# Selections of a graph layer's edge groups issued one step sooner, with half the descriptor store for POOL's gathers

## The chip, the cores and the metric

The kernel runs on one core of a Trainium2 chip. Its time is the device time of one execution in microseconds (us). Three runs of the kernel before took 1988.96, 1992.68 and 1994.04 us; their median is 1992.68. The engines are called PE (matrix products; PEld is its weight load), DVE (vector operations), ACT (activations and copies), POOL (here it only issues gathers) and SP (here it only issues DMAs). A queue name with a q, such as SPq, is an engine's list of DMA issues.

## The reference, cut to what matters

One message-passing layer on a graph of 12,500 nodes with 64 features and 200,000 edges with 32 features, the edges sorted by destination. All is float32.

```python
msg_in = concatenate([nodes[row], nodes[col], edge_features], axis=-1)   # 200000 x 160
messages = relu(msg_in @ mW1 + mb1) @ mW2 + mb2                          # hidden 128, out 64
aggregated = segment_sum(messages, col, num_segments=12500)
upd_in = concatenate([nodes, aggregated], axis=-1)
y = relu(upd_in @ uW1 + ub1) @ uW2 + ub2
out = layernorm(nodes + y)                                               # over 64 features
```

Here `row` is the source (`src`) and `col` the destination (`dst`) of an edge.

## The kernel before, in words

**Tiles, steps, supers.** An edge tile is 128 edges; there are 1563. A *step* `s` is 8 tiles (`SUB`), 196 steps in all; a *super* `g` is 16 tiles (`SUP`), two steps, 98 in all. In a step, `g, j = divmod(s, 2)`: j says whether it is the first or second step of its super.

**Tables.** The first product is split: `A = x @ mW1[source part]` and `B = x @ mW1[destination part] + mb1` are made once for all nodes and kept in DRAM (`tab_a`, `tab_b`). `chunk_a` makes 1024 rows of A: PE (L410), a copy by ACT (L420, half) and DVE (L418, half) into a tile `tb` with two buffers, and a DMA from ACT's queue (L422). There are 13 such pieces. The first 7 steps gather rows of x itself and multiply them (L236, L269); all later steps gather rows of A, so the first of those gathers waits until all 13 pieces are written.

**A step.** `gather(s)` issues 8 indirect DMAs on POOL (L168), each fetching the 128 source rows of a tile into `xg` (14 buffers). `edge_part(s)` lets PE compute the other two parts (L255): the left operand `l` holds, for each edge, its 32 edge features and a 32-row one-hot of its destination within a window of 32 nodes; the right operand `rhs` holds the weights of the edge features and the 32 rows of B of that window, which `windows(s)` fetches with 8 DMAs on SP (L229). `node_part(s)` adds the gathered rows (DVE L276) and applies the ReLU (ACT L277). `collect(s)` lets PE sum the messages by destination (L302) with the one-hot `sel` (edges x 32 nodes), and count edges (L307) with `selb`, its bfloat16 copy. Every few steps a period of up to 448 nodes is closed, updated, normalised and stored (`close`, `update`, `residual`, `norm`, `store`, with PE L337 to L347, ACT L339, DVE L351 to L364, SP L370).

**What a super's selection is.** `loadd(g)` fetches the destinations of 2048 edges into the one-hot rows of `l` (SP L184; three such operands in turn). `select(g)` runs on DVE: the node numbers (L194), the one-hot rows of `l` in place (L196), and `sel` (L200). `load(g)` fetches the edge features into the other rows of `l` (SP L215, two DMAs); for g > 2 it has to wait for L196, which writes all rows. `counts(g)` is ACT's copy to `selb` (L208). `sel` and `selb` come from the pool `sup`.

**What sets the order.** The order is written out by hand (`tc.manual_schedule()`): each engine runs its instructions in the order in which the loop `for s in range(last + 3)` issues them, and waits by semaphores. Before the loop the start issues 7 steps of gathers, the weights, the tables with some preparation put between pieces (`if k == ...`), and `relative`, which turns destinations into places within a window (L380). DMAs of SP and ACT complete on eight semaphores handed out in turn; each such DMA waits until the one that had its semaphore before has landed. POOL's gathers rotate over eight others in the same way.

In the kernel before, the loop issues `select`, `load` and `counts` of super g + 1 in the first step of super g, and `loadd` of super g + 2 in its second step. The store in SBUF for the descriptors of POOL's DMAs is set in the constructor at L779 (`dynamic_dma_scratch_size`), 32,768 bytes of each partition.

Of the kernel before, what the change touches and what calls it, by code (L numbers as in the profile page):

```python
# [26 lines left out]
NSUP = -(-NT // SUP)  # L27
# [39 lines left out]
def gnn_kernel(ctx: ExitStack, tc: tile.TileContext, x1T, x, eT, e_rows, src, dst, dst_row, wrow, wnext, whalf,  # L67
# [24 lines left out]
    nc = tc.nc  # L92
# [56 lines left out]
    def frees(s):  # L149

        a = (XG + 1) // 2 + s - XG - ROWB
        return min(2 * a + 1, XG - 1) if a < (XG + 1) // 2 else XG + a - (XG + 1) // 2
# [17 lines left out]
                in_offset=bass.IndirectOffsetOnAxis(ap=src_s[:, t:t + 1], axis=0))  # L170
        xg[s] = buf, a

    with tc.tile_pool(name="sup", bufs=2) as sup, tc.tile_pool(name="work", bufs=2) as work, tc.manual_schedule():
        L, S, SB, xs, hs, pcs, sums = {}, {}, {}, {}, {}, {}, {}
        pt = psum.tile([P, SUB // 2, P], F32, name="pt", tag="sums")

        def loadd(g):

            l = operand[g % 3]
            o = g * SUP * P  # L180
            dv = dst_row[:, o:o + SUP * P].rearrange("o (k b e) -> o b k e", b=2, e=P)
            for b in range(2):
                q = 64 * b + SK
                nc.sync.dma_start(l[q:q + WIN].bitcast(I32), dv[:, b].broadcast_to([WIN, SUP // 2, P]))  # L184
            L[g] = l

        def select(g):


            nt = min(SUP, NT - g * SUP)  # L190
            l = L[g]
            c = WIN + SUP // 2 * (g % 2)
            node = cps[:, c:c + SUP // 2]
            nc.vector.tensor_scalar(node, wh[:, g * SUP // 2:(g + 1) * SUP // 2], pidx, None, op0=ALU.add)  # L194
            for r in ([slice(0, P)] if g > 2 else [slice(SK, SK + WIN), slice(64 + SK, 64 + SK + WIN)]):
                nc.vector.tensor_tensor(l[r], l[r].bitcast(I32),  # L196
                                        node[r].unsqueeze(2).broadcast_to([r.stop - r.start, SUP // 2, P]),
                                        op=ALU.is_equal)
            s = sup.tile([P, SUP, WIN], F32, name="sel")
            nc.vector.tensor_tensor(s[:, :nt], slot.unsqueeze(1).broadcast_to([P, nt, WIN]),  # L200
                                    drc[:, g * SUP:g * SUP + nt].unsqueeze(2).broadcast_to([P, nt, WIN]),
                                    op=ALU.is_equal)
            S[g] = s

        def counts(g):
            nt = min(SUP, NT - g * SUP)
            sb = sup.tile([P, SUP, WIN], BF, name="selb")
            nc.scalar.copy(sb[:, :nt], S[g][:, :nt])  # L208
            SB[g] = sb

        def load(g):

            for b in range(2):
                q = 64 * b + EK
                nc.sync.dma_start(L[g][q:q + DE], eT[g, b])  # L215

        def windows(s):

            g = s // (SUP // SUB)
            o = s % (SUP // SUB) * SUB  # L220
            nt = len(tiles(s))
            r = rhs[g % 2]
            tab, n = (B0, EARLY - WIN + 1) if g < GE else (B, N)
            _, ws = nc.values_load_multi_w_load_instructions(
                wint[0:1, s * SUB:s * SUB + nt], engines=[ET.SP], min_val=0, max_val=n - 1,
                skip_runtime_bounds_check_because="destinations are node numbers")
            for i in range(nt):
                q = SK + 64 * (i % 2)
                nc.sync.dma_start(r[q:q + WIN, (o + i) // 2, :], tab[bass.ds(ws[i], WIN), :])  # L229
# [88 lines left out]
        def close(u):  # L318

            ps, pn = sums.pop(u)  # L320
            nc.scalar.copy(sums_s[u % 2], ps)  # L321
            nc.scalar.copy(xw[u % 2][0:1, :UW], pn)
# [52 lines left out]
        def relative(a, b):  # L375

            wbc = work.tile([P, WCH], I32, name="wbc", tag="tb")
            nc.sync.dma_start(dst_s[:, a:b], dst[:, a:b])
            nc.sync.dma_start(wbc[:, :b - a], wrow[:, a:b].broadcast_to([P, b - a]))
            nc.vector.tensor_tensor(drc[:, a:b], dst_s[:, a:b], wbc[:, :b - a], op=ALU.subtract)  # L380
# [33 lines left out]
        def chunk_a(c):  # L414
            pb, tb = products(c, w1a)
            for h, m in spread(c):
                if h:
                    nc.vector.tensor_copy(tb[:, h, :m], pb[:, h, :m])  # L418
                else:
                    nc.scalar.copy(tb[:, h, :m], pb[:, h, :m])  # L420
            n = min(NCH, NB - c)
            nc.scalar.dma_start(Av[:, c:c + n, :], tb.rearrange("p h i f -> p (h i) f")[:, :n])  # L422

        def chunk_b(c, into):
            pb, tb = products(c, w1b)
            n = min(NCH, NB - c)
            pf, tf = (t.rearrange("p h i f -> p (h i) f")[:, :n] for t in (pb, tb))
            nc.vector.tensor_tensor(tf, pf, b1.unsqueeze(1).broadcast_to([P, n, DH]), op=ALU.add)
            for v in into:
                nc.sync.dma_start(v[:, c:c + n, :], tf)  # L430

        def offsets():

            nc.vector.memset(usup[:, 0:1], 0)
            wv = wint.rearrange("o (s t) -> o s t", t=SUB)
            ov = woff.rearrange("o (s t) -> o s t", t=SUB)
            k = 0
            while k < K:
                end = UPD[k + 1:] + [NSUB]
                d = end[0] - UPD[k]  # L440
                n = 1
                while k + n < K and k and end[n] - UPD[k + n] == d:
                    n += 1
                if k:
                    nc.vector.tensor_copy(usup[:, k:k + n], wv[:, UPD[k]:UPD[k] + (n - 1) * d + 1:d, 0])
                w, o = (v[:, UPD[k]:UPD[k] + n * d].rearrange("o (n d) t -> o n (d t)", n=n) for v in (wv, ov))
                nc.vector.tensor_tensor(o, w, usup[:, k:k + n].unsqueeze(2).broadcast_to([1, n, d * SUB]),
                                        op=ALU.subtract)
                k += n
            nc.vector.tensor_tensor(ustep[:, 1:], usup[:, 1:], usup[:, :-1], op=ALU.subtract)  # L450
            for v in (woff, ustep[:, 1:]):
                nc.vector.tensor_scalar(v, v, 0.0, float(UW - WIN), op0=ALU.max, op1=ALU.min)
# [31 lines left out]
        for k, c in enumerate(range(0, NB, NCH)):  # L484
            chunk_a(c)
            if k == 0:
                chunk_b(0, [B0v, Bv])
            if k == 2:

                w0 = wint[:, :GE * SUP]  # L490
                nc.vector.tensor_scalar(past, w0[:, GE * SUP - 1:], float(EARLY - WIN), None, op0=ALU.is_gt)
                nc.vector.tensor_scalar(w0, w0, float(EARLY - WIN), None, op0=ALU.min)
                windows(0)
                windows(1)
            if k == 4:
                relative(0, 8 * SUP)
            if k == 6:
                offsets()
            if k == 9:
                select(0)  # L500
                load(0)
                counts(0)

        def rest(s):

# [77 lines left out]
        for s in range(last + 3):  # L583
            g, j = divmod(s, SUP // SUB)
            while gathered < NSUB and frees(gathered) < s:
                gather(gathered)
                gathered += 1
            if s - 2 in due:
                norm(due[s - 2])
            if s + 2 < NSUB:  # L590
                windows(s + 2)
            if s < NSUB:
                node_part(s)
            if 1 <= s <= NSUB:
                collect(s - 1)
            if s + 1 in due:
                close(due[s + 1])
            if j == 0 and g + 1 < NSUP:
                select(g + 1)
                load(g + 1)  # L600
                counts(g + 1)
            if j == 1 and g + 2 < NSUP:
                loadd(g + 2)
            if chunks and s >= BS and chunks[0] < NCH + NB * (s + 1 - BS) / (SUP // SUB * (GE - 1) - BS):
                chunk_b(chunks.pop(0), [Bv])
            if s + 1 < NSUB:
                if s + 1 < XG:
                    transpose(s + 1)
                edge_part(s + 1)
            if s in due and due[s] + 1 < K:  # L610
                carry(due[s] + 1)
            if s in due:
                update(due[s])
            if s - 1 in due:
                residual(due[s - 1])
            if s + 2 in due:
                columns(due[s + 2])
            rest(s)
            if s - 2 in due:
                store(due[s - 2])  # L620
# [166 lines left out]
```

## Time and profile before

| | |
|---|---|
| median of three runs | 1992.68 us |
| the profiled execution | 1992.68 us, its span 1990.9 us |
| granted TensorE clock, mean | 0.537 |
| gathers from the table (POOL L168) | 1507, 0.944 us each, first at 85.4, last at 1966.4 |
| `select`: DVE L196 / L200 | 98 supers, 1.22 us (128 rows) / 0.68 us |
| ACT L208 | 98, 0.62 us |
| adding gathered rows (DVE L276) | 190, 1.22 us; idle ahead of it 1185.6 us in all |

Busy shares are averages over the whole span. "Idle before" is time in which an engine did nothing just ahead of an instruction, put down to what ended it; for an engine that does not set the pace it costs nothing. A line `A <- B: us, times, longest` says that A waited for B. In a timeline, a row is start, duration, engine, line, operation, tiles, count, and in brackets the idle time ahead of it. Times are from the start of the span.

### The profile page before, as it was taken

How to read it: one execution, taken by the hardware profiler on the slowest of the kernel's cores; microseconds unless marked ns; L12 is line 12 of the kernel's file. 1: busy time of each engine (PE TensorE's matmuls, PEld its weight loads, DVE VectorE, ACT ScalarE, POOL GpSimd, SP SyncE). 2: the span in 40 equal slices, each digit the busy share in tenths (PEclk: the TensorE clock that was granted, in tenths of full speed). 3: DMA queues.
4: the chain of work that ended last, by engine and by line, in shares of the span. 5: the costliest groups of instructions: out<-in, count | busy, mean ns of one | idle time of the engine just before them, and what ended most of it. 6: DMA issues, size and time to landing. Idle time of an engine off the chain costs nothing. (4 is left out here: it accounts for less than half of the span.)

```text
span 1990.9 us, 34069 instructions
## 1 busy us (share of the span) xinstructions
PE 1446.1 (73%) x9234; PEld 1276.3 (64%) x9234; DVE 538.9 (27%) x1013; ACT 342.0 (17%) x453; POOL 1477.4 (74%) x1572
## 2 busy tenths in 40 slices
PE   3688666765766766767767767777778778888797
PEld 2577666665655655656666666666667667767675
DVE  1424222222221222222222222222222223232222
ACT  0221111111111111111111111111111112121121
POOL 7577777777777777777777777777777777777773
PEclk8575555555555555555555555555555555555555
DMA  8645444433333333333333433333334333334341
GB/s 208 178 122 138 117 119 110 110 95 93 96 96 95 96 96 98 97 95 98 97 97 97 100 96 100 97 101 97 100 96 104 98 100 100 102 100 105 97 105 50
DMA packets 240741, 208.75 MB, mean 105 GB/s; under 512 B 76605, under 2 KB 207167, under 8 KB 240560
## 3 DMA queue, kind: packets, MB, share of 16 engines
q0 software_dynamic: 50016, 100.70, 20.6%
q1 hardware_dynamic: 175998, 96.93, 17.8%
q10 hardware_dynamic: 14546, 8.93, 1.7%
q8 instruction: 87, 1.43, 0.3%
q14 instruction: 94, 0.77, 0.1%
HBM read 188.50 MB, written 17.83 MB: 104 GB/s over the span
## 5 line engine op out<-in xcount | busy, mean ns | idle before, releaser
L168 POOL DMA_INDIRECT xg<-tab_a,src_s x1507 | 1423.0, 944 | 471.4 <-issue 448.3
L302 PEld LDWEIGHTS sums<-sel,h 128*128 128x128 f32 x3126 | 650.9, 315 | 362.5 <-ACT h L277 325.9
L302 PE MATMUL sums<-sel,h 128*128 128x32 f32 x3126 | 661.2, 385 | 296.4 <-ACT h L277 292.1
L276 DVE TENSOR_TENSOR h<-pc,xg 128x1024 f32<-128x1024 f32 (+1 forms) x190 | 230.8, 1215 | 1185.6 <-DMA xg<-tab_a,src_s 1163.2
L255 PE MATMUL pc<-rhs,l 64*128 64x128 f32 x3126 | 398.4, 426 | 94.2 <-DVE h L276 87.2
L277 ACT ACTIVATE h<-h 128x1024 f32<-128x1024 f32 (+1 forms) x190 | 199.2, 1049 | 1264.9 <-DVE h L276 1258.2
L255 PEld LDWEIGHTS pc<-rhs,l 64*128 64x128 f32 x3126 | 341.6, 314 | 111.4 <-DVE h L276 91.6
L196 DVE TENSOR_TENSOR l<-l,cps 128x1024 f32<-128x1024 int32 (+1 forms) x101 | 123.3, 1221 | 36.5 <-DMA l<-in_dst_row 23.9
L346 PE MATMUL py<-ux,xw 128*128 128x64 f32 x272 | 86.8, 422 | 28.4 <-DVE h L276 28.4
L337 PE MATMUL pu<-sums_s,w2u 128*128 128x448 f32 x68 | 63.3, 1034 | 55.5 <-DVE h L276 55.0
L346 PEld LDWEIGHTS py<-ux,xw 128*128 128x128 f32 x272 | 71.8, 323 | 36.9 <-DVE h L276 32.0
L347 PE MATMUL py<-u,hTu 128*128 128x64 f32 x272 | 85.5, 418 | 0.4 <-ACT hTu L339 0.4
L208 ACT CAST selb<-sel 128x512 bf16<-128x512 f32 x98 | 60.4, 616 | 104.0 <-DVE sel L200 100.4
L307 PE MATMUL cnt<-selb,one 128*1 128x32 bf16 x1563 | 74.9, 188 | 0.0
L347 PEld LDWEIGHTS py<-u,hTu 128*128 128x128 f32 x272 | 73.4, 329 | 0.6 <-ACT hTu L339 0.6
L200 DVE TENSOR_TENSOR sel<-cps,drc 128x512 f32<-128x512 f32 x98 | 66.8, 682 | 9.0 <-PE sums L302 8.9
L168 POOL DMA_INDIRECT xg<-in_x,src_s x56 | 53.4, 953 | 17.9 <-issue 16.8
L307 PEld LDWEIGHTS <-one 128*1 128x1 bf16 x1563 | 52.3, 83 | 18.9 <-issue 9.0
L338 PE MATMUL pu<-xw,uz 128*128 128x448 f32 x68 | 57.5, 950 | 0.0
L351 DVE BATCH_NORM_STATS2 st<-py 128x6 f32<-128x64 f32 x136 | 21.2, 218 | 131.7 <-PE py L347 131.7
L337 PEld LDWEIGHTS pu<-sums_s,w2u 128*128 128x128 f32 x68 | 17.0, 310 | 61.6 <-DVE h L276 60.9
L410 PE MATMUL pb<-w1a,xall 64*128 64x128 f32 x196 | 24.4, 424 | 38.7 <-DVE tb L418 25.8
(87 smaller groups left out, 425.7 us busy)
## 6 DMA issues: line engine op xcount, KB each, us to landing
l<-in_dst_row SPq DMA_DIRECT2D x196, 128.0 KB
l<-in_eT SPq DMA_DIRECT2D x196, 128.0 KB
rhs<-tab_b SPq DMA_DIRECT2D x1563, 16.0 KB
xg<-tab_a,src_s POOLq DMA_INDIRECT x1507
tab_b<-tb SPq DMA_DIRECT2D x13, 512.0 KB
tab_a<-tb ACTq DMA_DIRECT2D x12, 512.0 KB
out<-o SPq DMA_DIRECT2D x34, 128.0 KB
xw<-in_x1T SPq DMA_DIRECT2D x34, 113.8 KB
```

Source lines behind the costliest of these rows:

```text
L168: nc.gpsimd.indirect_dma_start(out=a[:, i, :] if s < XG else a[:, i // 2, i % 2, :], out_offset=None, in_=A[:, :] if s >= XG else x[:, :], ...
L196: nc.vector.tensor_tensor(l[r], l[r].bitcast(I32), node[r].unsqueeze(2).broadcast_to([r.stop - r.start, SUP // 2, P]), op=ALU.is_equal)
L200: nc.vector.tensor_tensor(s[:, :nt], slot.unsqueeze(1).broadcast_to([P, nt, WIN]), drc[:, g * SUP:g * SUP + nt].unsqueeze(2).broadcast_to( ...
L208: nc.scalar.copy(sb[:, :nt], S[g][:, :nt])
L255: nc.tensor.matmul(pc[:, b, k, :], L[g][q:q + 64, m, :], rhs[g % 2][q:q + 64, m, :], start=s >= XG or k == 0, stop=s >= XG)
L276: nc.vector.tensor_tensor(hf[:, m], pf[:, m], a[:, m], op=ALU.add)
L277: nc.scalar.activation(hf[:, m], hf[:, m], AF.Relu)
L302: nc.tensor.matmul(ps[:, bass.ds(ws[i], WIN)], h[:, i % 2, i // 2, :], S[g][:, k0 + i, :], start=False, stop=ends and i == n - 1)
L307: nc.tensor.matmul(pn[:, bass.ds(ws[i], WIN)], one, SB[g][:, k0 + i, :], start=False, stop=ends and i == n - 1)
L337: nc.tensor.matmul(pu, w2u, sums_s[u % 2][:, :UN], start=True, stop=False)
L346: nc.tensor.matmul(py[:, i], xw[u % 2][:, i * P:(i + 1) * P], ux, start=True, stop=False)
L347: nc.tensor.matmul(py[:, i], hT[:, i * P:(i + 1) * P], u2, start=False, stop=True)
```

## The change

Four edits. (1) The pool `sup` has three buffers in place of two, for `sel` and for `selb`. (2) The start also issues `select`, `load` and `counts` of super 1, right after those of super 0, between the tenth and the eleventh table piece. (3) In the loop, `loadd(g + 2)` goes from the second step of super g to its first, and `select`, `load`, `counts` from the first step (for super g + 1) to the second (for super g + 2), which is one step sooner for each super. (4) The constructor's argument for the descriptor store is dropped, so that its default holds, 16,384 bytes of each partition.

```diff
-    with tc.tile_pool(name="sup", bufs=2) as sup, tc.tile_pool(name="work", bufs=2) as work, tc.manual_schedule():
+    with tc.tile_pool(name="sup", bufs=3) as sup, tc.tile_pool(name="work", bufs=2) as work, tc.manual_schedule():
...
             if k == 9:
                 select(0)
                 load(0)
                 counts(0)
+                select(1)
+                load(1)
+                counts(1)
...
-            if j == 0 and g + 1 < NSUP:
-                select(g + 1)
-                load(g + 1)
-                counts(g + 1)
+            if j == 0 and g + 2 < NSUP:
+                loadd(g + 2)
             if j == 1 and g + 2 < NSUP:
-                loadd(g + 2)
+                select(g + 2)
+                load(g + 2)
+                counts(g + 2)
...
-    nc = bacc.Bacc("TRN2", target_bir_lowering=False, num_devices=1, dynamic_dma_scratch_size=32768)
+    nc = bacc.Bacc("TRN2", target_bir_lowering=False, num_devices=1)
```

## The prediction

> **What bounds the kernel now.** I read the page's busy rows first, then POOL's waits and its line, then the timeline of the start, where the change puts work ahead of a stage that others wait for, and last a stretch of the middle.
>
> ```profile
> PE 1446.1 (73%) x9234; PEld 1276.3 (64%) x9234; DVE 538.9 (27%) x1013; ACT 342.0 (17%) x453; POOL 1477.4 (74%) x1572
> ```
>
> PE and POOL are equally busy, so shares decide nothing. POOL's waits, in us, times, longest, and then its one line (ns least/median/most):
>
> ```profile
> POOL xg L168 <- issue: 465.1, 1526, 0.3
> POOL xg L168 <- DMA tab_a<-tb: 12.4, 1, 12.4
> POOL xg L168 <- DMA xg<-tab_a,src_s: 5.2, 17, 0.3
> ...
> L168 POOL DMA_INDIRECT xg<-tab_a,src_s x1507: 940/944/1781, 85.4 to 1966.4; - x189
> ```
>
> POOL starts the first gather from the table at 85.4 and the last at 1966.4: 1881.0 us for 1506 steps, 1.249 us each: 0.944 of work and 0.305 of "issue", with no wait over 0.3 us. The "waits" for xg are the same 0.3. So the time is three pieces: 85.4 until the table stands, 1881 of gathers at a fixed pace, 24.5 of tail. Everyone else waits for this: DVE's L276 waits 1163.2 us for gathers. The profiled execution took 1992.68 us, which is the median of the three runs shown; its span is 1990.9, so 1.8 lies around it.
>
> The start, ACT's and DVE's queues merged in time:
>
> ```profile
> 72.11 0.37 ACTq L422 DMA_DIRECT2D tab_a<-tb  x1
> 75.45 0.62 ACT L208 CAST selb<-sel 128x512 bf16<-128x512 f32 x1 [4.09 <-DVE sel L200]
> 75.97 0.58 ACT L420 COPY tb<-pb 128x512 f32<-128x512 f32 x1
> 77.31 0.37 ACTq L422 DMA_DIRECT2D tab_a<-tb  x1
> 77.77 0.59 ACT L420 COPY tb<-pb 128x512 f32<-128x512 f32 x1 [1.22 <-DVE tb L418]
> 79.11 0.37 ACTq L422 DMA_DIRECT2D tab_a<-tb  x1
> 82.06 0.37 ACT L420 COPY tb<-pb 128x256 f32<-128x256 f32 x1 [3.70 <-DMA tab_a<-tb]
> 82.46 0.37 ACTq L422 DMA_DIRECT2D tab_a<-tb  x1
> ...
> 79.00 0.22 DVE L194 TENSOR_SCALAR cps<-wh,pidx 128x8 f32<-128x8 int32 x1
> 79.25 2.47 DVE L196 TENSOR_TENSOR l<-l,cps 32x1024 f32<-32x1024 int32 x2
> 81.75 0.69 DVE L200 TENSOR_TENSOR sel<-cps,drc 128x512 f32<-128x512 f32 x1
> ...
> 85.36 0.94 POOL L168 DMA_INDIRECT xg<-tab_a,src_s  x1 [12.37 <-DMA tab_a<-tb]
> ```
>
> The reader is to see a chain: ACT waits for the selection of super 0 (75.45), then makes the last three table pieces; the third reuses the buffer of the first, so it waits for that piece to land (77.31 to 82.06: 4.75); it goes out at 82.46, and POOL, idle since 73, starts 2.90 later. Below it stand the rows of super 1's selection, which today runs after this chain needs DVE.
>
> **The change, part by part.**
>
> *Selection, load and count copy of super 1, moved into the start.* They go between super 0's and the three last table pieces. DVE: 0.22 + 2.47 + 0.69, from 79.00 to 82.44: 3.44 us, now at 75.41 to 78.85. ACT's second L208 waits for it, and ACT is in order: behind it stand L420, the DMA of the piece, and two more pieces; POOL waits for the last. In before L420 began 0.52 after its L208 began; so L420 goes from 75.97 to about 79.40, 3.43 later, and the piece's DMA from 77.31 to 80.74. No cover here: POOL has nothing else to do. What can give some back is the landing of that piece. ACT's waits for a piece sent before took, in order of time, 6.50 (27.57 to 34.07), 4.89, 3.85, 3.33 (46.83 to 50.16), 3.43 and this 4.75; with 4.75 again the shift is 3.4, with the shortest 2.0, with the longest 5.2. Today it goes out 1.9 us after a 512 KB load of destinations (SP L378, 75.38); afterwards the distance is about as in SP's list below, 3.5. I take 3.2, nearer the like-for-like 3.4.
>
> *SP in the start.* Each DMA of SP and ACT takes one of eight semaphores in turn and waits until the DMA that last held it has landed; moving DMAs deals these anew. In the changed program load(1) goes from 65.15 to right after load(0), 56.3; the destinations of super 2 from 74.42 to before the windows of step 3; the last window of step 3 then waits for the table piece sent at 72.11 (landing some 3.7 later, 75.8), and load(2) joins; so L378 moves from 75.38 to about 77.3. The three late table pieces wait for windows sent by 73.3, long landed at 80.7: 0. L379 needs the buffer of the piece sent at 79.11: it moves from 84.26 by the same 3.4, and the windows of step 4 with it. Behind it is PE's edge_part of step 4. Its cover: POOL reuses a buffer first at step 21, at 226.06, and DVE freed it at 119.7: 106 us. Cost 0; if that cover went, 3.4 would be lost once, not more, as POOL would wait once.
>
> *L380 beside a gather.* The gather at 87.86 took 1.78 us, 0.84 over the rest, while DVE ran L380 (87.60, 1.23 long). L380 shifts with the stream. It may miss a gather or hit one fully: -0.84 to +0.39; I take 0.
>
> [...]
>
> *Selections one step sooner in the loop.* 98 of each (DVE L194, L196, L200; ACT L208; two loads on SP) before and after, so nothing is removed. What moves is the step: the middle looks like this.
>
> ```profile
> 1007.61 0.94 POOL L168 DMA_INDIRECT xg<-tab_a,src_s  x1 [0.30 <-issue]
> 1007.69 0.22 DVE L194 TENSOR_SCALAR cps<-wh,pidx 128x8 f32<-128x8 int32 x1
> 1007.95 1.22 DVE L196 TENSOR_TENSOR l<-l,cps 128x1024 f32<-128x1024 int32 x1
> 1008.86 0.94 POOL L168 DMA_INDIRECT xg<-tab_a,src_s  x1 [0.31 <-issue]
> 1009.08 0.68 DVE L200 TENSOR_TENSOR sel<-cps,drc 128x512 f32<-128x512 f32 x1
> ...
> SPq L215 <- DVE l L196: 572.6, 89, 9.0
> ```
>
> The gathers keep 0.94 beside all three. SP stands 6.4 us (572.6 / 89) in each super behind L196; queued behind are the next eight windows, used two steps (20 us) later, and PE's L255 appears nowhere as waiting for them. That wait only changes its step; a row store (L370) or column load (L330) that falls in the same step now stands behind it or no longer does, and POOL waits for neither. DVE's wait for PE to free a selection (L200, 8.9 us in all) goes; nothing is late next, as POOL waits for none of them. Cover: POOL's pace. Cost 0. In the tail nothing moves: the last selection (L200 at 1947.78) goes about 10 us further from it.
>
> *Half the descriptor store, a third selection buffer.* Buffers cost only room (sel 2 KB, selb 1 KB a partition). The store isn't an operation in the trace, so it is bounded. POOL's own instructions are the same. Its gathers also rotate over eight semaphores, each waiting for the eighth before it, so at most eight are unfinished, whatever the store's size. Lower row: 42 early gathers, with the store still fresh (starts 10.51 to 62.96), have a mean pace of 1.2488, a thousand late ones (715.44 to 1963.90) 1.2485, and after the 59th no step is over 1.262: 0, and no gain either, since a store with little in it was no cheaper. Upper, from the nearest odd row: if the smallest store that holds eight had to be turned round with a stall of 0.84 (the stretched gather), 1563/8 x 0.84 = 164 us. I take 0, the row of 1500 like gathers.
>
> [...]
>
> Sum: 1992.68 + 3.2 = **1995.9**; bounds without the store +1.2 (2.0 - 0.84) to +5.6 (5.2 + 0.39).
>
> **The rivals.**
> (a) Forecast: POOL starts 3.2 late, same pace: 1995.9. For it: the chain at 75 to 85.
> (b) The start swallows it: pieces land sooner because SP's transfers are out of the way, or chip noise in the start covers it: 1992.7. Against: ACT's order is fixed; the shortest landing leaves 2.0.
> (c) Slower: the smaller store makes each gather dearer (POOL must look for or await room at L168). Each ns costs 1.5 us; from 1.9 ns it passes +0.3% (1998.7); one per cent of the pace, 12.5 ns, gives 2014.7. Against: filling the store had no price.
> (d) Faster: part of the 0.305 between gathers is care for the store and shrinks with it; 10 ns give 1980.8, from 6 ns it counts. Against: the same row. Or the sooner selection is worth something after all: L208's 100.4 and L200's 8.9 us of waits could bring up to 109 (1887) if on the path; POOL's waits say they aren't.
>
> **How the numbers follow.** (a) 0.60, (b) 0.12, (c) 0.18, (d) 0.10. A measurement here tells about 0.3% (6.0 us) from no change; the three runs themselves span 5.1. (a) and (b) lie within: same 0.72, slower 0.18, faster 0.10. The range: (a)'s own is 1990.2 (fastest run, 1988.96 + 1.2) to 1999.6 (slowest, 1994.04 + 5.6), whose last microsecond is counted with (c); (b) takes it to 1989; (c) with up to 1.6 ns a gather adds 2.4, to 2002. Left out are the rest of (c) and (d).
>
> **What would show it.** First gather from the table at 88 to 89 instead of 85.4; two L208 in a row before 80; pace 1.249, last gather 1881 after the first; tail 24.5. The prediction is wrong if the pace differs by over 2 ns, if POOL shows a wait over 1 us after 90, or if the first gather starts before 86.

## The result and the profile after

The changed kernel takes 1996.62 us (median; 1993.32 to 2000.54) where the kernel before took 1992.15 (1988.96 to 1994.54). The ratio is 1.0023, 95% interval 1.0014 to 1.0032, which is 2.8 to 6.4 us: slower, by less than the 0.3% that was named as the line between a change and none. The profiled execution took 1994.01 us, its span is 1992.2.

The page's busy row, then POOL's waits and its line, of the kernel after:

```profile
PE 1439.2 (72%) x9234; PEld 1270.8 (64%) x9234; DVE 538.7 (27%) x1013; ACT 342.0 (17%) x453; POOL 1477.4 (74%) x1572
```

```profile
POOL xg L168 <- issue: 479.3, 1524, 15.1
POOL xg L168 <- DMA xg<-tab_a,src_s: 7.9, 26, 0.3
...
L168 POOL DMA_INDIRECT xg<-tab_a,src_s x1507: 940/944/1952, 88.3 to 1969.3; - x189
```

The counts of instructions are those of before. POOL's longest wait is one of 15.1 us, now put down to "issue"; it is the same wait for the table that stood under `tab_a<-tb` before, and what it was put down to changed because the semaphore of the last piece is now the first of several that POOL reads one after the other (in the trace the gather starts 0.97 us after that semaphore, 0.79 in the kernel before). The line shows the shift: the first gather at 88.3, the last at 1969.3, both 3.0 later, so 1881.0 us lie between them again.

The start, ACT's, DVE's, SP's and POOL's rows:

```profile
71.73 0.37 ACTq L422 DMA_DIRECT2D tab_a<-tb  x1
75.06 0.62 ACT L208 CAST selb<-sel 128x512 bf16<-128x512 f32 x1 [4.09 <-DMA tab_a<-tb]
78.52 0.62 ACT L208 CAST selb<-sel 128x512 bf16<-128x512 f32 x1 [2.84 <-DVE sel L200]
79.04 0.58 ACT L420 COPY tb<-pb 128x512 f32<-128x512 f32 x1
80.38 0.37 ACTq L422 DMA_DIRECT2D tab_a<-tb  x1
...
82.18 0.37 ACTq L422 DMA_DIRECT2D tab_a<-tb  x1
83.75 0.37 ACT L420 COPY tb<-pb 128x256 f32<-128x256 f32 x1 [2.32 <-DMA tab_a<-tb]
84.15 0.37 ACTq L422 DMA_DIRECT2D tab_a<-tb  x1
...
75.33 2.45 DVE L196 TENSOR_TENSOR l<-l,cps 32x1024 f32<-32x1024 int32 x2
77.79 0.69 DVE L200 TENSOR_TENSOR sel<-cps,drc 128x512 f32<-128x512 f32 x1
...
77.14 0.42 SPq L378 DMA_DIRECT2D drc<-in_dst  x1
87.06 0.35 SPq L379 DMA_DIRECT2D wbc<-in_wrow  x1
...
88.34 0.94 POOL L168 DMA_INDIRECT xg<-tab_a,src_s  x1 [15.06 <-issue]
```

Two L208 stand in a row, and ACT idles 2.84 us ahead of the second, for super 1's selection. Everything that makes the last three pieces comes after it.

The spans of the six kernels profiled where the kernel before takes 1992 to 1996 us, in three pieces (start, gathers, tail), each from one profiled execution. The sixth column is the stretch of gathers beside L380, told of at the end; the seventh is the gathers' piece without it.

| kernel | first gather from the table | last one | between | tail | beside L380 | between, less that |
|---|---|---|---|---|---|---|
| before | 85.36 | 1966.39 | 1881.03 | 24.5 | 0.84 | 1880.2 |
| after | 88.34 | 1969.30 | 1880.96 | 22.9 | 1.01 | 1880.0 |
| ring_half | 84.61 | 1965.03 | 1880.42 | 25.4 | 0.29 | 1880.1 |
| start_only | 88.84 | 1968.75 | 1879.91 | 24.1 | 0 | 1879.9 |
| sel_only | 89.74 | 1973.64 | 1883.90 | 22.8 | 0.22 | 1883.7 |
| start_late | 86.86 | 1970.69 | 1883.83 | 24.1 | 0.03 | 1883.8 |

The two profiled spans differ by 1.28 us: 2.98 from the start, -0.07 from the gathers and -1.63 from the tail. The medians differ by 4.5. Single executions differ by some 3.7 us in the gathers' pace and some 2.6 in the tail, whatever the kernel, so the whole is read by the ratios' intervals. The first gather is a better measure of the start, but not an exact one: with the same start it comes 0.75 apart in before and ring_half, and 1.40 apart in after and sel_only. The cleanest is the time on ACT from the table piece sent just ahead of the change to the next one. It is 5.20 in before (72.11 to 77.31), 5.19 in ring_half and in start_late, and 8.65 (71.73 to 80.38), 8.65 and 8.66 in after, start_only and sel_only: 3.45 us more wherever super 1's selection stands there.

### The profile page after: what moved, and what is told of

Same layout as the page of the kernel before. It is cut to its first block, busy times and chain, and to the rows that moved or that the text cites. A ratio compares the mean times of both kernels' runs of the same rounds, so it can differ in the third digit from the quotient of the medians.

```text
span 1992.2 us, 33425 instructions
## 1 busy us (share of the span) xinstructions
PE 1439.2 (72%) x9234; PEld 1270.8 (64%) x9234; DVE 538.7 (27%) x1013; ACT 342.0 (17%) x453; POOL 1477.4 (74%) x1572
## 5 line engine op out<-in xcount | busy, mean ns | idle before, releaser
L276 DVE TENSOR_TENSOR h<-pc,xg 128x1024 f32<-128x1024 f32 (+1 forms) x190 | 230.8, 1215 | 1197.0 <-DMA xg<-tab_a,src_s 1153.9
L255 PE MATMUL pc<-rhs,l 64*128 64x128 f32 x3126 | 393.4, 424 | 78.0 <-DVE h L276 77.4
L196 DVE TENSOR_TENSOR l<-l,cps 128x1024 f32<-128x1024 int32 (+1 forms) x101 | 123.3, 1221 | 23.4 <-DMA l<-in_dst_row 20.1
L208 ACT CAST selb<-sel 128x512 bf16<-128x512 f32 x98 | 60.4, 616 | 94.4 <-DVE sel L200 89.9
L200 DVE TENSOR_TENSOR sel<-cps,drc 128x512 f32<-128x512 f32 x98 | 66.8, 682 | 0.1
L410 PE MATMUL pb<-w1a,xall 64*128 64x128 f32 x196 | 24.1, 417 | 41.7 <-DVE tb L418 28.5
## 6 DMA issues: line engine op xcount, KB each, us to landing
xw<-in_x1T SPq DMA_DIRECT2D x34, 113.8 KB
```

Of the source, the lines that this page charges most:

```text
L196: nc.vector.tensor_tensor(l[r], l[r].bitcast(I32), node[r].unsqueeze(2).broadcast_to([r.stop - r.start, SUP // 2, P]), op=ALU.is_equal)
L255: nc.tensor.matmul(pc[:, b, k, :], L[g][q:q + 64, m, :], rhs[g % 2][q:q + 64, m, :], start=s >= XG or k == 0, stop=s >= XG)
L276: nc.vector.tensor_tensor(hf[:, m], pf[:, m], a[:, m], op=ALU.add)
```

## The experiments

The theory: the only part of the change that costs is super 1's selection in the start; it makes POOL's first gather from the table late, and the gathers' fixed pace carries that to the end. Rivals: the smaller store makes gathers dearer; the sooner selection in the loop costs or brings something.

The first four ran beside the kernel before at a median of 1995.55 us (1993.27 to 1998.77). The later ones came to chips on which the kernel before had medians of 2744 to 2792 us; in a profile of it taken on one of them (before_again, below) eight window loads of SP take 18.57 us in a stretch, where they took 4.18 in before. These chips are called slowly served here. The time of each of those is compared with the kernel before on its own chip and with nothing else.

### The store alone

```diff
 before:
-    nc = bacc.Bacc("TRN2", target_bir_lowering=False, num_devices=1, dynamic_dma_scratch_size=32768)
+    nc = bacc.Bacc("TRN2", target_bir_lowering=False, num_devices=1)
```

> The kernel before with the descriptor store of 16,384 bytes alone. Start theory (the whole loss is POOL's later first gather from the table): no difference, 1992 us, ratio 1.000 within the interval, first gather near 85.4, pace 1.2485 us. Store theory (the smaller store makes gathers dearer): the whole loss is here, 1996.5 us, with the pace at about 1.2515 or single long gathers that recur. If the loss is shared, something between.

Measured: 1994.16 us, ratio 0.9999 (0.9990 to 1.0008). First gather at 84.61. Half the store has no price that the time can show: the upper end of the interval is 1.6 us over 1507 gathers, about 1 ns each, and rival (c) began to count at 1.9. The traces show a very small one, some 10 ns for each turn of the store, told of at the end.

### Super 1's selection in the start alone

```diff
 before:
             if k == 9:
                 select(0)
                 load(0)
                 counts(0)
+                select(1)
+                load(1)
+                counts(1)
...
-            if j == 0 and g + 1 < NSUP:
+            if j == 0 and 0 < g and g + 1 < NSUP:
```

> The kernel before, store of 32,768 bytes and loop as before, but super 1's selection, load and count copy are issued in the start right after super 0's (and left out of step 0). Start theory: all of the loss, 1995 to 1997 us, ratio 1.0015 to 1.0025, first gather from the table about 3 us later, near 88.4. Store theory and loop theory (the sooner selections cost something in the loop or the tail): 1992 us and ratio 1.000.

Measured: 1998.38 us, ratio 1.0016 (1.0007 to 1.0025), 1.4 to 5.0 us. The loop and the store are those of before, and the loss is there. ACT's and POOL's rows of this kernel:

```profile
79.33 0.62 ACT L208 CAST selb<-sel 128x512 bf16<-128x512 f32 x1 [2.84 <-DVE sel L200]
79.85 0.58 ACT L420 COPY tb<-pb 128x512 f32<-128x512 f32 x1
81.19 0.37 ACTq L422 DMA_DIRECT2D tab_a<-tb  x1
...
84.95 0.37 ACTq L422 DMA_DIRECT2D tab_a<-tb  x1
...
88.84 0.94 POOL L168 DMA_INDIRECT xg<-tab_a,src_s  x1 [15.46 <-DMA tab_a<-tb]
```

The same 2.84 of waiting ahead of the second L208, and the first gather 3.5 later than before.

### The change with the old store

```diff
 after:
-    nc = bacc.Bacc("TRN2", target_bir_lowering=False, num_devices=1)
+    nc = bacc.Bacc("TRN2", target_bir_lowering=False, num_devices=1, dynamic_dma_scratch_size=32768)
```

> The changed kernel with the store of 32,768 bytes: parts one to three of the change without the fourth. Start theory: as the changed kernel, 1995 to 1997 us, ratio 1.0015 to 1.0025. Store theory: 1992 us, ratio 1.000.

Measured: 1998.88 us, ratio 1.0019 (1.0010 to 1.0029). The store given back brings nothing, and against start_only on the same chip the moved loop adds 0.5 us (1998.88 - 1998.38), which the intervals can't tell from zero. The first gather comes at 89.74.

### Super 1's selection behind the last piece

```diff
 after, in the start:
             if k == 9:
                 select(0)
                 load(0)
                 counts(0)
-                select(1)
-                load(1)
-                counts(1)
+
+        select(1)
+        load(1)
+        counts(1)
```

> The changed kernel (small store, three buffers, selections one step sooner in the loop), but super 1's selection, load and count copy stand after the last table piece instead of before the last three. Start theory: the loss is gone, 1992 us, ratio 1.000, first gather near 85.4. Loop theory and store theory: still 1996 us, ratio 1.0015 to 1.0025, though the first gather is back at 85.4.

Measured: 1998.54 us, ratio 1.0014 (1.0005 to 1.0023). The expectation of no loss was missed, and beside sel_only (1998.88) the times show no gain from taking the selection out of the start. The trace says why in part. Rows of ACT, SP and POOL of this kernel:

```profile
77.15 0.37 ACTq L422 DMA_DIRECT2D tab_a<-tb  x1
...
83.11 0.37 ACT L420 COPY tb<-pb 128x256 f32<-128x256 f32 x1 [4.91 <-DMA tab_a<-tb]
83.52 0.37 ACTq L422 DMA_DIRECT2D tab_a<-tb  x1
...
76.09 0.88 SPq L215 DMA_DIRECT2D l<-in_eT  x2
77.01 0.42 SPq L378 DMA_DIRECT2D drc<-in_dst  x1
...
86.86 0.95 POOL L168 DMA_INDIRECT xg<-tab_a,src_s  x1 [13.72 <-issue]
```

ACT is as early as in the kernel before (77.15 against 77.31), but its piece is waited out only after 5.96 us instead of 4.75: SP's 512 KB of destinations (L378), which went out at 75.38 before, goes out at 77.01, 0.14 ahead of the piece, with two edge loads just ahead of that. So the first gather is still 1.5 late, which lies within the interval of 1.0 to 4.6 us. The selection's own share in the start went; a second cost, of the loads that the change moves on SP, took its place. In the trace's packets the data of these loads moves from 77.14 to 81.2, and the first packet of the piece starts only at 79.25, 2.1 after its issue, where it took 1.1 before; in the changed kernel that data is done at 80.4, as the piece is sent (80.38) and ahead of its first packet (81.28). Two later traces, told of under start_late_rel, show the landing with L378 beside the piece and without it.

### Two kernels again, and one with a later preparation

The start_late and sel_only traces had a back-to-back pace of 1.2509 us where the other four had 1.2483 to 1.2486. Over 1506 steps that is 3.7 us, as much as the effect looked for. To see whether it belongs to the kernels, three were profiled again (no edit).

> The kernel before once more, unchanged, for a second profile of it. Two profiles of the runs so far (both loop parts with the large store, and the late selection) had a gather pace of 1.2509 us from the first gather on, four had 1.2483 to 1.2486; 2.5 ns a gather are 3.8 us. If the pace belongs to the single execution, this one may show either. If it belongs to the program, it shows 1.2485 again.

> The selections one step sooner with the store of 32,768 bytes, unchanged, for a second profile. If the pace of the gathers belongs to the program: 1.2509 us again. If to the execution: either value, 1.2484 as likely as before.

> The late selection of super 1, unchanged, for a second profile. If the pace belongs to the program: 1.2509 us again. If to the execution: either value. The table piece sent at 77.15 took 5.96 us to be waited out beside the load of destinations sent at 77.01 on SP; if that collision is the cause of the late first gather (86.86), it recurs here: 86 to 87.

Measured: 2773.5, 2772.59 and 2782.36 us, beside 2757.63 to 2804.66 for the kernel before there; no verdict on the times. The paces of gathers that follow each other without a wait were 1.2507, 1.2482 and 1.2481: all three turned over, the kernel before to the longer and the other two to the shorter value. The pace is not fixed by the kernel, and both paces came up on the same chip; it is no part of the change.

These traces also show what else is different on such a chip. POOL's waits in before_again:

```profile
POOL xg L168 <- issue: 434.0, 1397, 6.8
POOL xg L168 <- DVE h L276: 324.4, 59, 12.1
POOL xg L168 <- DVE cps L194: 307.5, 59, 10.9
POOL xg L168 <- DMA tab_a<-tb: 61.0, 1, 61.0
```

POOL waits 632 us for DVE there, so the gathers' own pace no longer sets the time. The same eight window loads of SP, in the kernel before on the first chip and then here:

```profile
1010.82 4.18 SPq L229 DMA_DIRECT2D rhs<-tab_b  x8
```

```profile
1402.88 18.57 SPq L229 DMA_DIRECT2D rhs<-tab_b  x8
```

They take 18.57 us instead of 4.18. In that stretch of the trace SP's register operations, which wait for no semaphore, often stand 0.7 us or more behind the instruction ahead of them, where those of before have 0.02 to 0.05 among its eight loads; that instructions reach the engine slowly is a reading of this, and what makes them late isn't shown.

A version meant to beat both kernels moves all of the preparation behind the last piece, in place of super 1's alone:

```diff
 after, in the start:
-            if k == 4:
-                relative(0, 8 * SUP)
-            if k == 6:
-                offsets()
-            if k == 9:
-                select(0)
-                load(0)
-                counts(0)
-                select(1)
-                load(1)
-                counts(1)
+
+        relative(0, 8 * SUP)
+        offsets()
+        select(0)
+        load(0)
+        counts(0)
+        select(1)
+        load(1)
+        counts(1)
```

> The changed kernel with all that stands between table pieces in the start (the places of the first edges L378 to L380, the offsets L434 to L452, the selections, loads and count copies of supers 0 and 1) moved after the last piece. Start theory: the pieces no longer wait for this work (10 us of offsets, selection and the wait for destinations lie between them), the table stands before or soon after the gathers of x end at 73, the first gather from the table comes at 73 to 77 instead of 88, and the time falls by 9 to 13 us against the kernel before: 1980 to 1984, ratio 0.9935 to 0.9955, since the first steps have over 100 us before POOL needs a buffer of theirs. If the late work is in the way of something else (the first steps pace the gathers after all), the gain is lost: 1992 or more.

> The same kernel as prep_late (changed loop, small store, all work between the table pieces moved after the last piece), once more, since the chip of the earlier run served the engines' instructions far slower (the kernel before took 2792 us there). On a chip like the first two. Start theory: the first gather from the table at 73 to 77 instead of 85.4, the pace one of 1.2484 or 1.2509, the tail 23 to 25, so the time is 8 to 12 us under the kernel before, ratio 0.994 to 0.996. If the sooner selections or the small store cost 3 us of their own in the loop, only 5 to 9 us, ratio 0.9955 to 0.9975. If the first steps pace the gathers, no gain.

> The start alone is changed against the changed kernel: the relative numbers, the offsets and both selections with their loads and counts stand behind the last piece of the table. Theory of the start (the gathers of the table pace the rest, so every microsecond by which the first one comes sooner is one off the whole): on a chip where the kernel before takes some 1993 us, the first gather of the table comes at 73 to 77 us where it came at 85.4, and the ratio is 0.994 to 0.996. If the loop's sooner selection or the smaller store costs some 3 us of its own: 0.9955 to 0.9975. If the first steps' other work paces the gathers instead, the first comes sooner, a wait of as much follows it, and the ratio is 1.000. On a chip where the kernel before takes 2745 to 2790 us: 0.985 to 0.99 as in the two runs before, and the question of its worth on the other chips stays open.

Measured, on three chips of the slowly served kind: 2752.38 us, ratio 0.9887 (0.9854 to 0.9920); 2703.79 us, 0.9864 (0.9828 to 0.9901); 2750.14 us, 0.9879 (0.9849 to 0.9909). The first gather from the table, in before_again and then in prep_late_3:

```profile
133.75 0.94 POOL L168 DMA_INDIRECT xg<-tab_a,src_s  x1 [61.03 <-DMA tab_a<-tb]
```

```profile
117.41 0.94 POOL L168 DMA_INDIRECT xg<-tab_a,src_s  x1 [44.66 <-DMA tab_a<-tb]
```

It comes 16.3 us sooner, while the ratio is worth 34 us (0.0121 x 2785.8). If all of that is kept to the end, which no run shows where POOL also waits for DVE, the start accounts for half; where the rest comes from is open. What it is worth where the kernel before takes 1993 us wasn't measured.

### The relative numbers one step later

```diff
 start_late, in rest(s):
-            if s == 1:
+            if s == 2:
                 relative(8 * SUP, 8 * SUP + WCH)
-            elif s == 2:
+            elif s == 3:
                 relative(8 * SUP + WCH, NT)
```

> As the late selection of super 1 (changed loop, small store), and also the second and third loads of destinations with their L380 (relative) are issued one step later each, so that SP sends no 512 KB load beside the last table pieces. Collision theory (what was left of the loss with the late selection was that load beside the piece sent at 77.15, which took 5.96 us instead of 4.75): first gather from the table at 85.4 or a little sooner, and the time of the kernel before, ratio 0.999 to 1.0005. Loop theory (the sooner selections themselves cost 2 to 3 us in the loop or the tail): still 1.0010 to 1.0020, with the first gather at 85.4.

Measured: 2768.35 us, ratio 0.9943 (0.9919 to 0.9966), some 16 us faster than the kernel before on that chip, though its first gather from the table comes at 135.50, no sooner than before_again's 133.75. It was meant to take L378 out of the way of the last pieces. On this chip the whole time can't answer for that, but the traces do. ACT's and SP's rows of start_late_again, with L378 beside the piece, and then ACT's of start_late_rel, without it:

```profile
126.78 0.41 ACTq L422 DMA_DIRECT2D tab_a<-tb  x1
132.21 0.37 ACT L420 COPY tb<-pb 128x256 f32<-128x256 f32 x1 [4.34 <-DMA tab_a<-tb]
...
126.79 0.42 SPq L378 DMA_DIRECT2D drc<-in_dst  x1
```

```profile
127.38 0.37 ACTq L422 DMA_DIRECT2D tab_a<-tb  x1
130.91 0.37 ACT L420 COPY tb<-pb 128x256 f32<-128x256 f32 x1 [2.48 <-PE pc L255]
```

The piece is waited out after 5.43 us with L378 beside it, much as start_late's 5.96, and after 3.53 without it; from the piece to the first gather it is 9.31 (to 136.09) and 8.12 us (to 135.50). So it is L378 that makes the landing long, as far as one execution of each, on two chips, can show. The edge loads (L215) go out just ahead of the piece in both. The edit also moves the loads behind L378 (L379, L385), which did not stand beside this piece in either.

The run shows, besides, a gain that is not from the start. It is as large as the half of prep_late's that was left over, and both kernels have the changed loop, whose selection comes a step sooner where POOL waits for DVE; but the changed kernel itself wasn't timed against before on such a chip, and that reading is only argued.

### A store too small to go unnoticed

```diff
 before:
-    nc = bacc.Bacc("TRN2", target_bir_lowering=False, num_devices=1, dynamic_dma_scratch_size=32768)
+    nc = bacc.Bacc("TRN2", target_bir_lowering=False, num_devices=1, dynamic_dma_scratch_size=1024)
```

> The kernel before with a descriptor store of 1,024 bytes of each partition, a thirty-second of its own. If the store's size has no price because at most eight gathers are unfinished, and in fact two to three (a gather lands 2.1 to 3.4 us after its start at a pace of 1.25): ratio 1.000, pace 1.2484 or 1.2509. If POOL has to wait for room or to clear it: a longer gather every few, 0.84 us each or more, 1563/8 x 0.84 = 164 us or more, over 2150.

Measured: 2816.71 us, ratio 1.010 (1.0064 to 1.0136). Where gathers follow each other from the start, POOL's rows of this kernel show two late gathers that the kernel before doesn't have:

```profile
9.27 0.94 POOL L168 DMA_INDIRECT xg<-in_x,src_s  x1 [0.30 <-issue]
10.51 0.94 POOL L168 DMA_INDIRECT xg<-in_x,src_s  x1 [0.30 <-issue]
12.46 0.95 POOL L168 DMA_INDIRECT xg<-in_x,src_s  x1 [1.01 <-issue]
13.71 0.94 POOL L168 DMA_INDIRECT xg<-in_x,src_s  x1 [0.30 <-issue]
...
21.20 0.96 POOL L168 DMA_INDIRECT xg<-in_x,src_s  x1 [0.30 <-issue]
22.66 0.94 POOL L168 DMA_INDIRECT xg<-in_x,src_s  x1 [0.51 <-issue]
```

The first seven gathers have no such wait; the eighth comes 1.95 after the seventh (10.51 to 12.46), and the sixteenth is late again. Neither expectation (1.000, or over 2150 us) was met. A store so small costs here, and what the rows show of it is waiting, which rival (c) named beside dearer gathers. That it is waiting for room is only argued: by the trace's packets the first gather had landed at 10.95, ahead of the eighth's turn at 11.76, and three gathers were unfinished at the sixteenth. Of the 1% in all, these two waits are under 1 us (0.71 and 0.21), and turning the store round adds some 2 (195 gathers at 10 ns, see the end); in the rest POOL waits for DVE and the table as the kernel before does on such chips, and what makes the whole longer stays open.

An estimate: by the spacing of the longer gathers in before and after a gather takes up 144 bytes of the store (worked out at the end), so 1,024 bytes hold seven, and the late eighth gather agrees with that.

## Why the prediction was right

The forecast was 1995.9 us and slower-than-before by less than 0.3%; the median is 1996.62. Step by step:

- **The bound.** Right: 1881.03 us of gathers before, 1880.96 after, steps without a stretched gather 1.2485 and 1.2483 on average, and no wait over 0.32 us after the first. The 3 us that the start loses are lost at the end.
- **ACT behind super 1's selection.** Right: 3.45 us from one piece's issue to the next, in three traces, where 3.43 was worked out. L420 moved by only 3.07 (75.97 to 79.04) because this execution was 0.38 ahead already at the piece before the change (72.11 against 71.73); that is the execution's, not the change's.
- **The landing of the pieces.** Mis-sized twice, in opposite directions. The step kept the landing nearly the same ("nearer the like-for-like 3.4"). The piece sent at 80.38 was waited out by 83.75, 3.37 us instead of 4.75, a gain of 1.4; the last piece, whose landing the sum left as it was at 2.90, took until 88.34, 4.19, a loss of 1.3. The two belong together: sent sooner, the last piece stands behind more of the piece ahead of it. In the trace's packets 493 packets (of 512 bytes) of the earlier pieces had yet to start when it went out, 67 in the kernel before. So the sooner buffer gave almost nothing back, and from the first of these three pieces to the gather it takes 7.96 us after and 8.05 before. The range's lower end, 2.0 by the shortest landing, counted on that gain and left this out. The sum came out as 3.45 - 0.38 - 1.38 + 1.29 = 2.98; that it stands so close to 3.2 owes something to luck. start_only has the same two: 81.19 to 84.55 and 84.95 to 88.84.
- **SP in the start at cost 0.** The places were right (L378 foreseen at about 77.3, found at 77.14; L379 at about 87.7, found at 87.06). The price is hidden by the selection, which the prediction did not say: with the selection taken away from ACT, start_late's piece meets that very L378, and its first gather is still 1.5 late. In the changed kernel the selection delays the piece past the load, whose packets end at 80.4. The two costs don't add.
- **Selections one step sooner in the loop.** Right: sel_only and start_only are 0.5 us apart.
- **Half the store.** Right: ring_half's ratio is 0.9999. The upper bound of 164 us had nothing behind it: a turn of the store costs some 10 ns, not 0.84 us, and the halved store has six more gathers that run over its end, 0.06 us in all.
- **L380 beside a gather, between -0.84 and +0.39.** It went from 0.84 to 1.01, that is +0.17.
- **The tail of 24.5.** 22.9 in this execution, and 22.8 to 25.4 in six kernels whose tails do the same work; the prediction took it as fixed. In the profiled execution this gave back 1.6 of the 3.0.

Of the rivals, (b) is out in its plain form (the first gather did move), (c) by ring_half, (d) by the unchanged pace and ring_half. The start's 3.0 lies in the whole's interval of 2.8 to 6.4 us; whether there is more to the loss than the start isn't shown. The median moved by 4.5, and the executions' own spread in pace (3.7) and tail (2.6) is of the size of the remainder.

## What to carry to other kernels

Where one engine runs at a fixed pace from its first piece of work to the end, as POOL did here (1881.0 us of gathers before and after), the one thing to look for in a change is what it puts ahead of that first piece (3.45 us on ACT here); the loop took the moving for nothing (0.5 us between sel_only and start_only). When a step is moved, the transfers that it moves on another queue can have their own effect on what lands beside them, and taking the visible cause away can uncover them, as in start_late, whose piece was waited out after 5.96 us instead of 4.75. A transfer that lands sooner need not give anything back: here the first of the last three pieces took 1.4 us less to be waited out, and the last one 1.3 more until POOL started. And half the descriptor store cost nothing here that the times can show (ratio 0.9999), while one of 1,024 bytes made the kernel 1% slower (1.010).

## What the runs showed of the hardware that was not expected

**Gathers that began well inside L380 ended 0.81 or 0.82 us after it.** L380 subtracts two operands that both lie in SBUF. The rows of before and after beside it (the bracket is idle time ahead):

```profile
87.60 1.23 DVE L380 TENSOR_TENSOR drc<-drc,wbc 128x1024 f32<-128x1024 int32 x1 [5.16 <-DMA wbc<-in_wrow]
...
87.86 1.78 POOL L168 DMA_INDIRECT xg<-tab_a,src_s  x1 [0.30 <-issue]
```

```profile
90.75 1.22 DVE L380 TENSOR_TENSOR drc<-drc,wbc 128x1024 f32<-128x1024 int32 x1 [5.24 <-DMA wbc<-in_wrow]
...
90.84 1.95 POOL L168 DMA_INDIRECT xg<-tab_a,src_s  x1 [0.31 <-issue]
```

In the kernel after, the gather that begins 0.09 into L380 ends 0.82 after it (92.79 against 91.97). In the kernel before the one that began 0.26 into it ended 0.81 after it (89.64 against 88.83), and so in each of the other traces where a gather began between 0.09 and 1.08 us into an L380: 0.81 or 0.82, ten cases in all. Gathers that began in its first 0.03 or its last 0.08 us kept their 0.94. So the first 0.13 us of a gather (0.944 less 0.81) seem not to be held, and 0.81 follow once DVE's line is done. In the six traces of the table, 2857 gathers from the table ran beside L196, L200 or L276, which read one operand from PSUM, and not beside L380; none took over 0.957.

L380 is not alone. L452, in the offsets of the start, has one operand, in SBUF, and two constants, and a gather that began in it ended as long after it (rows of after):

```profile
65.20 1.02 DVE L452 TENSOR_SCALAR woff<-woff 1x1568 int32<-1x1568 int32 x1
...
65.73 1.30 POOL L168 DMA_INDIRECT xg<-in_x,src_s  x1 [0.30 <-issue]
```

The gather ends 0.81 after L452 (67.03 against 66.22); in prep_late, where L452 runs beside a gather from the table, it is 0.82.

So gathers beside lines with one operand in PSUM took 0.957 us at most, and those that began inside L380 or L452, with operands in SBUF alone, up to 1.95 and 1.30 in after. That the place of the operands decides it, no run shows.

**The turn of the descriptor store shows in single gathers.** In before six gathers took 949 to 962 ns, from the 228th to the 1366th, 227.6 gathers apart on average. In after, with half the store, twelve did, from the 114th to the 1480th, 113.8 apart, if the one double distance (911th to 1138th) counts twice. An estimate from this: 32,768 bytes over 227.6 and 16,384 over 113.8 are both 144 bytes for each gather, and the gather missing in the double distance, the 1024th, would end just where the store does. Counted so from the first gather on, the gathers that run over the store's end take 949 to 962 ns in each of the fourteen traces, where the others have a median of 944 (947 in executions of the longest pace). There are 6 such gathers with 32,768 bytes (median 954 in before), 12 with half of that (953 in after and in ring_half) and 195 in ring_1024 (953); counts of 112, 160 or 176 bytes pick out no longer gathers there. So the traces agree with the estimate, and a turn costs some 10 ns.

**The pace of back-to-back gathers is held through an execution and differs between executions**, also of the same kernel: 1.2481 to 1.2485 us in seven of fourteen traces, 1.2507 to 1.2509 in four, and 1.2493 (ring_1024), 1.2496 (prep_late_3) and 1.2503 (prep_late_2) in between. On this kernel the difference is up to 4 us, 0.2%. What chooses the value is not known.

**The same kernel took 40% longer on another chip** (a median of 2792.34 us on before_again's, 1992.15 beside the changed kernel). SP's window loads took 18.57 us in a stretch of before_again where they took 4.18 in before, with the gathers at nearly the same pace between waits (1.2507 and 1.2485). A ratio measured in one of these conditions says little about the other: start_late was 1.0014 on the chip of the first four, and start_late_rel, the same but for one step's loads, 0.9943 on the other.
